# A four-layer graph network on one core: the last chunk's dense products in two column halves, and 0/1 patterns in the last head's first part

## The chip, the core and the metric

The kernel runs on one core of one Trainium2 chip. A core has a matrix engine (TensorE, PE in the profile), a vector engine (VectorE, DVE), an activation engine (ScalarE, ACT), GpSimd (POOL) and SyncE (SP), which here only starts transfers. The metric is the device time of one launch in microseconds. Before the change three runs took 1820.46, 1822.46 and 1822.22 us, median 1822.22.

## The reference, cut to what matters

There are 2708 nodes with 512 features each and a dense 0/1 adjacency matrix. Four layers follow one another, each added to its own input. `lrelu` is a leaky ReLU, `first64` keeps the first 64 neighbors of every row.

```python
def ln_relu(x): return maximum(layernorm(x), 0)

h = ln_relu(x)                                   # layer 0: graph convolution
x = x + relu((adj.T @ h @ W0) * (1/sqrt(degree))[:, None])

h = ln_relu(x)                                   # layer 1: mean of the first 64 neighbors
nb = (first64(adj) @ h) / count
x = x + lrelu(h @ W_line.T + b_line) + lrelu(nb @ W_nb.T + b_nb)

h = ln_relu(x)                                   # layer 2: attention, 8 heads of 64 columns
Wh = h @ W2[head];  f1 = Wh @ a1[head];  f2 = Wh @ a2[head]
e = where(adj > 0, lrelu(f1[:, None] + f2[None, :], 0.2), -9e15)
x = x + concat_over_heads(elu(softmax(e) @ Wh))

h = ln_relu(x)                                   # layer 3: mean of all neighbors
agg = (adj @ h) / degree
x = x + relu(concat(h @ W_self + b_self, agg @ W_nb + b_nb) @ W_comb + b_comb)
```

## The kernel before, in words

**Tiling.** The nodes are cut into 22 chunks of R = 126 rows. The last chunk has 62 rows only; its tiles are loaded twice, into partitions 0 to 61 and again into 64 to 125 (TAIL = 64), so that both copies run through layer norm, transposition and product. The 512 features are four blocks of 128 (NF). The chunks are also taken in groups of 3 or 4 as output columns of the adjacency.

**Layers 0, 1 and 3** have the same two stages. In the dense stage each chunk of the input is loaded, normalized (`norm`, L186), transposed with a ReLU (`relu_T`, L208), and multiplied with the 512x512 weight by `product` (L182): four float32 matmuls, one for each block of features, each 512 columns wide. (Each float32 matmul leaves two records in the trace, so a product is eight.) The product is then cut by `halves` (L258) into a rounded part and the rest[...]. For a full chunk the two parts are two tiles of 126x512; for the last chunk they share one tile, `tail`: the rounded part in rows 0 to 61, the rest in rows 64 to 125, so that one matmul takes both (L366).

The aggregation stage (`aggregate`, L376) multiplies with the adjacency: for each group of output chunks it runs over the 22 input chunks, and the adjacency block for a step (`kt`, made by VectorE in `weight1` L739 and `weight3` L1294) is prepared two steps ahead in three buffers. Layer 0 has one such product (`product0`, L443), layer 1 two (`product1`, L714, with weights `wn` and `wl`), layer 3 two (`nb3`, L1253, and `self3`, L1258; their weights `wfn` and `wfs` are fused from W_nb, W_self and W_comb at the start of the kernel). In layer 1 and 3 the second product does not go into the aggregation: a bias and, in layer 1, a leaky ReLU are applied (`y`), and the rows are stored to DRAM.

**Layer 2.** A dense stage (`product2`, L919) gives Wh, stored to DRAM, and from products with the rows `arow` the two scores f1 and f2. Its first steps run within the aggregation of layer 1. Then ten units of attention follow: head 0 in two parts (1384 and 1324 nodes), heads 1 to 6 whole, head 7 in two parts. Units are numbered from 0, so the first part of the last head is unit 8. Each unit has 22 steps, one for each chunk of neighbors. In a step

- VectorE makes the weights `t` (`make`, L880, one instruction at L886), three steps ahead, in TILES = 4 buffers;
- ScalarE scales the chunk's Wh by exp(f2) (`scale`, L868);
- TensorE multiplies both (`multiply`, L1077): `av`, the weighted sum of Wh, and `sums`, the softmax's denominator. Since an output has only 64 + 1 rows, the nodes are cut into parts that use 32 columns of the array each, four side by side.

The denominator has two forms. In the plain one it is a float32 matmul with exp(f2) itself in one column (`one6`, L876). For 13 of the 22 chunks (BY_SIDE, L795: m mod 5 in 1, 3, 4), where `by_side` (L809) says so, it is a bf16 matmul instead: ScalarE makes a 0/1 pattern `b` of the places where one branch of the leaky ReLU holds (`compare`, L897, a steep sigmoid), and `multiply_sides` (L1092) multiplies it with exact three-part splits of the scores (`parts`). What the other branch adds is counted once for all heads over the same 13 chunks (`mask` L1138, `count_neighbors` L1145, with `parts2`), and the three are put together in layer 3 (`turn3`, L1015). Before the change `by_side` holds for heads 1 to 6.

**Order.** The order is written out by hand and each engine works through its own queue in it. `staged` (L217) interleaves the stages of a dense loop; in the attention, `plan` and `behind` (L1182 to L1222) put other work behind given steps (loading the next head's row, the count, storing results by `evict` L1102, the first chunks of layer 3), and the loop at L1224 emits it all. SyncE starts most loads and stores, ScalarE and GpSimd some. A tile that is allocated in a pool reuses the buffer of an older tile of its tag, and its first write waits until the older one has been read.

The functions of the change:

Of the kernel before, what the change touches and what calls it, by code (L numbers as in the profile page):

```python
# [8 lines left out]
F32 = mybir.dt.float32  # L9
# [11 lines left out]
P = 128  # L21

R = 126
# [21 lines left out]
def fast_layers(  # L45
# [129 lines left out]

    def load_row(pool, src, name, tag=None):

        t = pool.tile([P, D], F32, name=name, tag=tag or name)
        nc.sync.dma_start(t, bass.AP(tensor=src.tensor, offset=src.offset, ap=[[0, P], [1, D]]))
        return t  # L180

    def product(po, lhsT, w, n):  # L182
        for f in range(NF):
            nc.tensor.matmul(po[:n], lhsT[:, f, :n], w[:, f, :], start=(f == 0), stop=(f == NF - 1))  # L184

    def norm(xc, n, scalar=False):  # L186
# [71 lines left out]
    def halves(ring, po, c):  # L258

        if c < NC - 1:  # L260
            t = ring.tile([R, 2, D], F32R, name="halves")
        else:
            t = ring.tile([R, 1, D], F32R, name="tail", bufs=1)
        nc.scalar.copy(t[:, 0, :], po[:R])
        if c < NC - 1:
            nc.vector.tensor_tensor(t[:, 1, :], po[:R], t[:, 0, :].bitcast(F32), ALU.subtract)
        else:
            second = t[TAIL : TAIL + last_rows, 0, :]
            nc.vector.tensor_tensor(
                second, po[TAIL : TAIL + last_rows], second.bitcast(F32), ALU.subtract  # L270
            )
        return t

# [143 lines left out]
    with ExitStack() as ring_ctx:  # L417
# [25 lines left out]
        def product0(c, xc, hT, n):  # L443
            po = ps.tile([P, D], F32, name="h0_ps", tag="ps")
            product(po, hT, w0s, n)
            h0[c] = halves(ring, po, c)
# [267 lines left out]
        def product1(c, xc, hT, size):  # L714
            n = rows(c)
            pn = ps.tile([P, D], F32, name="nb_ps", tag="ps")
            product(pn, hT, wn, size)
            h1[c] = halves(ring, pn, c)
            po = ps.tile([P, D], F32, name="line_ps", tag="ps")
            product(po, hT, wl, size)  # L720
            y = common.tile([P, D], F32, name="y", tag="t", bufs=3)
            nc.vector.tensor_tensor(y[:n], po[:n], bl[:n], ALU.add)
            nc.vector.scalar_tensor_tensor(
                y[:n], y[:n], SLOPE1, y[:n], op0=ALU.mult, op1=ALU.max
            )
            nc.gpsimd.tensor_tensor(xc[:n], xc[:n], y[:n], ALU.add)
            move(nc.scalar, x1[c * R : c * R + n, :], xc[:n])

# [80 lines left out]
    def by_side(u, m):  # L809
        return 0 < units[u][0] < H - 1 and m in BY_SIDE  # L810

# [15 lines left out]
    parts_of = parts[:, : NC * H * 8].rearrange("p (m h k) -> p m h k", h=H, k=8)  # L827
    parts2 = at.tile([R, NC, H, 3], BF16, name="parts2")
    nc.gpsimd.memset(parts2, 0.0)
# [306 lines left out]
    counted, masks = [], {}  # L1136

    def mask(i, j):  # L1138
        m = BY_SIDE[i]
        q = rows(m)  # L1140
        g, k = where[m]
        t = masks[i, j] = common.tile([P, D], F32, name="x", bufs=XBUFS).bitcast(BF16)
        nc.scalar.copy(t[:q, :quarter], vT[g][:q, k, j * quarter : (j + 1) * quarter])

    def count_neighbors(i):  # L1145
        m = BY_SIDE[i]
        q = rows(m)
        if i == 0:
            counted.extend(
                ps.tile([P, 512], F32, name="adj_sums", tag="ps") for _ in pieces(quarter)  # L1150
            )
# [12 lines left out]
        for p, (a, b) in zip(counted, pieces(quarter)):  # L1164
            t = common.tile([P, D], F32, name="out", tag="t", bufs=3)
            for j in range(4):
                own = slice(j * S, j * S + 3 * H)
                nc.scalar.copy(t[own, : b - a], p[own, : b - a])
                nc.sync.dma_start(
                    sumT[7 * H :, j * quarter + a : j * quarter + b], t[own, : b - a]  # L1170
                )
# [72 lines left out]
    with ExitStack() as stack:  # L1244
        ring = stack.enter_context(tc.tile_pool(name="ring3", bufs=NC - 1, reuse_waits="tile"))
        b3 = e3.tile([P, D], F32, name="b3", bufs=1)
        nc.sync.dma_start(
# [5 lines left out]
        def nb3(c):  # L1253
            pn = ps.tile([P, D], F32, name="nb3_ps", tag="ps")
            product(pn, kept3[c][1], wnb, R)
            h3[c] = halves(ring, pn, c)

        def self3(c):  # L1258
            n = rows(c)
            po = ps.tile([P, D], F32, name="self_ps", tag="ps")  # L1260
            product(po, kept3.pop(c)[1], wself, R)
            y = common.tile([P, D], F32, name="y", tag="t", bufs=3)
            ins = nc.vector.tensor_tensor(y[:n], po[:n], b3[:n], ALU.add)
            move(nc.scalar, s3[c * R : c * R + n, :], y[:n])
            return ins.ins
# [713 lines left out]
```

## Time and profile before

The profiled execution took 1820.7 us, of which the span from the first to the last instruction is 1818.8 us. The table splits the span by stages; busy times are sums over the instructions of an engine within that stretch.

| stage | stretch, us | PE busy | DVE busy | ACT busy |
|---|---|---|---|---|
| fused weights, layer 0 | 0 to 376 | 361.3 | 267.4 | 214.9 |
| layer 1 dense | 376 to 541 | 162.2 | 82.4 | 32.1 |
| layer 1 aggregation | 541 to 769 | 225.6 | 144.6 | 6.2 |
| layer 2 dense | 769 to 854 | 84.5 | 67.2 | 51.9 |
| attention, ten units | 854 to 1411 | 551.3 | 538.8 | 388.0 |
| layer 3 dense | 1411 to 1589 | 175.3 | 123.3 | 104.8 |
| layer 3 aggregation | 1589 to 1818 | 221.4 | 84.3 | 0.0 |

How to read it: the difference between a stretch and an engine's busy time is that engine's idle time there. In the attention, TensorE and VectorE are both busy almost throughout; elsewhere VectorE has room. A mean duration of an instruction in the profile is the time from its start to its end, and since matmuls overlap in the array it is longer than the time from one start to the next; the latter is what one more matmul costs. The clock that the chip granted to TensorE, as a mean over the span, was 0.996 of full speed.

### The profile page before, as it was taken

The numbers are of one execution on the slowest core, as the hardware profiler recorded it, in microseconds if no ns is written. First come the engines' busy times: TensorE is split into PE (matmuls) and PEld (weight loads), VectorE is DVE, ScalarE is ACT, GpSimd is POOL, SyncE is SP. The second block draws the span as 40 slices with busy tenths as digits, with TensorE's granted clock in tenths as the row PEclk, the third lists the DMA queues.
The fourth block names the chain that finished last, engine by engine and source line by source line (L and its number), as shares of the span: only waits on it lengthen the run. The fifth ranks groups of instructions, "written<-read, shape, count | busy, mean of one in ns | idle before, by whom it ended". The sixth has DMA issues, their size and how long they took to land.

```text
span 1818.8 us, 30698 instructions
## 1 busy us (share of the span) xinstructions
PE 1781.6 (98%) x11884; PEld 1036.1 (57%) x11884; DVE 1307.9 (72%) x1836; ACT 798.0 (44%) x1542; POOL 245.3 (13%) x241
## 2 busy tenths in 40 slices
PE   9899999999999999999999999999999999999998
PEld 4456777654447887644444344444444454488776
DVE  4942998955546655888999999999998777533334
ACT  2642777722110000156887767767744566400000
POOL 0101333301121111266000000000001222100000
PEclk9999999999999999999999999999999999999999
DMA  7632666635461211343221121122022444313221
GB/s 248 193 114 67 204 208 196 204 76 121 117 149 55 67 54 46 97 147 104 73 61 26 42 62 43 27 61 57 13 65 56 134 131 139 94 38 102 78 69 45
DMA packets 165554, 176.63 MB, mean 97 GB/s; under 512 B 94830, under 2 KB 115792, under 8 KB 164516
## 3 DMA queue, kind: packets, MB, share of 16 engines
q1 hardware_dynamic: 143170, 131.47, 26.2%
q10 hardware_dynamic: 18484, 33.28, 5.4%
q0 software_dynamic: 3744, 9.82, 1.6%
q8 instruction: 96, 1.57, 0.4%
q14 instruction: 60, 0.49, 0.1%
HBM read 111.35 MB, written 55.15 MB: 92 GB/s over the span
## 4 chain that ended last, share of the span: by engine, by line
PE 80%; DVE 9%; issue 4%; DMA 4%; ACT 1%; POOL 1%; SPq 0%; DVEq 0%; ACTq 0%; POOLq 0%
PE acc L368 31%; PE av L1069 19%; PE nb_ps L184 7%; PE sums L1069 6%; PE self_ps L184 4%; PE wh_ps L184 3%; DVE t L886 3%; PE line_ps L184 3%; DVE cum L494 2%; PE h_ps L184 2%; PE hT_ps L212 2%; PE fused_ps L312 2%; DMA x<-x 1%; DMA ai<-in_adj 1%; DVE two L506 1%
## 5 line engine op out<-in xcount | busy, mean ns | idle before, releaser
L886 DVE SCALAR_TENSOR_TENSOR t<-rb,ec,vT 126x2708 f32<-126x2708 f32 (+2 forms) x220 | 532.2, 2472 | 17.6 <-PE sums L1069 9.7
L368 PE MATMUL acc<-halves,kt 126*126 126x512 f32 x1848 | 435.9, 395 | 3.9 <-DVE kt L741 2.3
L1069 PE MATMUL av<-t,whs 126*32 126x451 f32 (+3 forms) x4576 | 436.2, 515 | 0.6 <-DVE ln_mv L191 0.6
L368 PEld LDWEIGHTS acc<-halves,kt 126*126 126x126 f32 x1848 | 342.6, 186 | 93.7 <-DVE kt L741 6.9
L1069 PEld LDWEIGHTS av<-t,whs 126*32 126x32 f32 (+1 forms) x4576 | 158.7, 110 | 207.8 <-issue 188.0
L368 PE MATMUL acc<-halves,ar 126*126 126x512 f32 x924 | 232.7, 405 | 2.1 <-DVE deg L502 1.1
L904 ACT ACTIVATE b<-t,eb 126x2708 bf16<-126x2708 f32 (+1 forms) x78 | 199.1, 2552 | 25.4 <-DVE t L886 25.1
L368 PEld LDWEIGHTS acc<-halves,ar 126*126 126x126 f32 x924 | 169.1, 186 | 52.7 <-issue 7.7
L193 ACT ACTIVATE ln_rs<-ln_mv,eps 126x1 f32<-126x1 f32 x88 | 25.6, 293 | 339.5 <-DVE ln_mv L191 336.5
L741 DVE SCALAR_TENSOR_TENSOR kt<-lastr,index,vT 126x504 fp32r<-126x504 int16 (+3 forms) x154 | 110.6, 729 | 81.0 <-PE acc L368 80.7
L1296 DVE CAST kt<-vT 126x504 fp32r<-126x504 uint8 (+3 forms) x154 | 56.0, 366 | 138.2 <-PE acc L368 138.2
L1069 PE MATMUL sums<-t,whs 126*32 126x338 f32 (+5 forms) x1568 | 139.6, 449 | 2.4 <-ACT out L1110 2.4
L874 ACT ACTIVATE whs<-wh,ef 126x64 f32<-126x64 f32 x220 | 76.8, 349 | 130.6 <-PE sums L1069 66.1
L1036 POOL TENSOR_SCALAR z<-y 126x512 f32<-126x512 f32 x22 | 44.0, 2000 | 662.2 <-DVE y L1029 653.4
L494 DVE TENSOR_TENSOR_SCAN cum<-ai,deg 126x504 int16<-126x504 int32 (+2 forms) x110 | 128.6, 1182 | 0.5 <-DMA ai<-in_adj 0.5
L522 ACT ACTIVATE cum<-cum,limit 126x504 int16<-126x504 int16 (+3 forms) x132 | 88.2, 668 | 58.4 <-DVE deg L502 57.3
L1069 PEld LDWEIGHTS sums<-t,whs 126*32 126x32 f32 (+1 forms) x1568 | 54.9, 109 | 70.0 <-issue 43.7
L189 DVE BATCH_NORM_STATS2 ln_st<-x 126x6 f32<-126x512 f32 x88 | 60.4, 686 | 43.1 <-DMA x<-x 29.1
L184 PE MATMUL h_ps<-w0s,hT 128*126 128x512 f32 x176 | 79.7, 596 | 6.0 <-ACT hT L214 4.7
L184 PE MATMUL nb_ps<-wfn,hT 128*126 128x512 f32 x176 | 81.7, 608 | 2.0 <-ACT hT L214 2.0
L184 PE MATMUL wh_ps<-w2s,hT 128*126 128x512 f32 (+1 forms) x176 | 79.4, 593 | 0.0
L184 PE MATMUL nb_ps<-wn,hT 128*126 128x512 f32 x176 | 79.2, 592 | 0.0
(182 smaller groups left out, 1869.8 us busy)
## 6 DMA issues: line engine op xcount, KB each, us to landing
x<-x SPq DMA_DIRECT2D x105, 252.0 KB
x<-x ACTq DMA_DIRECT2D x84, 252.0 KB
ai<-in_adj SPq DMA_DIRECT2D x84, 249.0 KB
x<-in_x SPq DMA_DIRECT2D x42, 252.0 KB
rb<-rT SPq DMA_DIRECT2D x7, 1332.8 KB
wh<-whd SPq DMA_DIRECT2D x70, 94.5 KB
packed<-two POOLq DMA_DIRECT2D x44, 124.5 KB, 4.3
whd<-wh SPq DMA_DIRECT2D x21, 252.0 KB
```

What stands on the lines that cost most here:

```text
L184: nc.tensor.matmul(po[:n], lhsT[:, f, :n], w[:, f, :], start=(f == 0), stop=(f == NF - 1))
L189: nc.vector.bn_stats(st[:n], xc[:n])
L368: nc.tensor.matmul(acc[:R], weight[:, k * R : (k + 1) * R], parts[:, i, :], start=(m == 0 and i == 0), stop=(m == NC - 1),)
L494: nc.vector.tensor_tensor_scan(cum[:n, :gw], ai[:n, :gw], ai[:n, :gw], 0.0 if g == 0 else deg[:n, m : m + 1], op0=ALU.add, op1=ALU.max,)
L522: nc.scalar.activation(cum[:n, :gw], cum[:n, :gw], AF.Sign, bias=limit[:n], scale=-1.0, accum_out=signs[:n, m, g : g + 1],)
L741: nc.vector.scalar_tensor_tensor(by_chunk(kt, cs), lastr[:, cs[0] * R : (cs[-1] + 1) * R].rearrange("p (c r) -> p c r", r=R), index[:R, m ...
L874: ins = nc.scalar.activation(t[:q, :O], wh.pop((u, m))[:q], AF.Copy, scale=by)
L886: ins = nc.vector.scalar_tensor_tensor(t[:q, : hi - lo], row[h][:q, lo:hi], ec[:q, m, h : h + 1], vT[g][:q, k, lo:hi], op0=ALU.max, op1=AL ...
L904: nc.scalar.activation(b[:q, : hi - lo], weight[s][:q, : hi - lo], AF.Sigmoid, bias=eb[:q, m, h : h + 1], scale=STEEP,)
L1036: nc.gpsimd.tensor_scalar(z, y, 0.0, None, op0=ALU.min)
L1069: nc.tensor.matmul(p[j * S : (j + 1) * S, : b - a], lhsT, rhs[:, part * size + a : part * size + b], start=(s % NC == 0), stop=(s % NC == ...
L1296: nc.vector.tensor_copy(by_chunk(kt, cs), pattern(m, cs))
```

## The change

It has three parts. Everything else is as before.

**Products of the last chunk.** Where a dense product is for the last chunk, `product_of_last` takes only the 62 rows once and cuts the 512 output columns into two halves. The first half is written to rows 0 to 61 of the result, the second to rows 64 to 125, by two matmuls of 256 columns that use different columns of the array. `any_product` chooses; it is used by all six products. What follows is adapted: `halves` for the last chunk clears the `tail` tile and fills it by three copies and two subtractions, `product1` and `self3` do their bias, leaky ReLU and stores in two corners, and `product2` copies two corners.

**Patterns in one more unit.** `by_side` holds for unit 8 as well, for the same 13 chunks. `parts2` now exists in two forms, for the first half of the nodes (heads 1 to 7) and for the second (heads 1 to 6), filled by six copies; the count is cut at the same node as head 7's parts (`fourths`).

**Tiles moved.** The rows `arow` are loaded into a tile of the `weights` pool with tag `w` instead of their own; `rest` uses a tile with tag `t`; `b3` is allocated in the ring of layer 3. By these pools some loads and a few VectorE instructions come at another place in their queues: the `arow` loads go earlier, `wfs` later (behind the last product of layer 2, as `wfn`), `b3` behind the last stores of the attention; one `kt` cast of layer 1 stands ahead of the reductions of `w2s` (L772), and the first three casts of layer 3 ahead of the last `hn` (L203).

```diff
-    def load_row(pool, src, name, tag=None):
-
-        t = pool.tile([P, D], F32, name=name, tag=tag or name)
+    def load_row(pool, src, name, into=None):
+
+        t = into
+        if t is None:
+            t = pool.tile([P, D], F32, name=name)
...
+    HALF = D // 2
+
+    corners = [
+        (slice(0, last_rows), slice(0, HALF)),
+        (slice(TAIL, TAIL + last_rows), slice(HALF, D)),
+    ]
+
+    def product_of_last(po, lhsT, w):
+
+        for f in range(NF):
+            for at_rows, at_cols in corners:
+                nc.tensor.matmul(
+                    po[at_rows, at_cols],
+                    lhsT[:, f, :last_rows],
+                    w[:, f, at_cols],
+                    start=(f == 0),
+                    stop=(f == NF - 1),
+                )
+
+    def any_product(c, po, lhsT, w, n):
+        if c == NC - 1:
+            product_of_last(po, lhsT, w)
+        else:
+            product(po, lhsT, w, n)
...
-        nc.scalar.copy(t[:, 0, :], po[:R])
         if c < NC - 1:
+            nc.scalar.copy(t[:, 0, :], po[:R])
             nc.vector.tensor_tensor(t[:, 1, :], po[:R], t[:, 0, :].bitcast(F32), ALU.subtract)
-        else:
-            second = t[TAIL : TAIL + last_rows, 0, :]
-            nc.vector.tensor_tensor(
-                second, po[TAIL : TAIL + last_rows], second.bitcast(F32), ALU.subtract
-            )
-        return t
+            return t
+        nc.gpsimd.memset(t.bitcast(F32), 0.0)
+        (low, first), (high, other) = corners
+        t = t[:, 0]
+        nc.scalar.copy(t[low, first], po[low, first])
+        nc.scalar.copy(t[low, other], po[high, other])
+        nc.scalar.copy(t[high, other], po[high, other])
+        nc.vector.tensor_tensor(
+            t[high, first], po[low, first], t[low, first].bitcast(F32), ALU.subtract
+        )
+        nc.vector.tensor_tensor(
+            t[high, other], po[high, other], t[high, other].bitcast(F32), ALU.subtract
+        )
+        return t.rearrange("p (i d) -> p i d", i=1)
...
-            product(po, hT, w0s, n)
+            any_product(c, po, hT, w0s, n)
...
-            product(pn, hT, wn, size)
+            any_product(c, pn, hT, wn, size)
...
-            product(po, hT, wl, size)
+            any_product(c, po, hT, wl, size)
...
-            nc.vector.tensor_tensor(y[:n], po[:n], bl[:n], ALU.add)
-            nc.vector.scalar_tensor_tensor(
-                y[:n], y[:n], SLOPE1, y[:n], op0=ALU.mult, op1=ALU.max
-            )
-            nc.gpsimd.tensor_tensor(xc[:n], xc[:n], y[:n], ALU.add)
-            move(nc.scalar, x1[c * R : c * R + n, :], xc[:n])
+            for own in corners if c == NC - 1 else [(slice(0, n), slice(0, D))]:
+                nc.vector.tensor_tensor(y[own], po[own], bl[own], ALU.add)
+                nc.vector.scalar_tensor_tensor(
+                    y[own], y[own], SLOPE1, y[own], op0=ALU.mult, op1=ALU.max
+                )
+                nc.gpsimd.tensor_tensor(xc[own], xc[own], y[own], ALU.add)
+                move(nc.scalar, x1[c * R : c * R + n, own[1]], xc[own])
...
-        return 0 < units[u][0] < H - 1 and m in BY_SIDE
+        return 1 < u < len(units) - 1 and m in BY_SIDE
...
-    parts2 = at.tile([R, NC, H, 3], BF16, name="parts2")
+    parts2 = at.tile([R, len(BY_SIDE), 2, H, 3], BF16, name="parts2")
...
-    ar = [load_row(pp, a, f"arow{i}") for i, a in enumerate((a1, a2))]
+    arows = weights.tile([P, NF, D], F32, name="arows", tag="w")
+    ar = [load_row(None, a, None, into=arows[:, i]) for i, a in enumerate((a1, a2))]
...
-        product(po, hT, w2s.rearrange("p f h o -> p f (h o)"), n)
+        any_product(c, po, hT, w2s.rearrange("p f h o -> p f (h o)"), n)
         wh = pp.tile([R, D], F32, name="wh", bufs=3)
-        nc.scalar.copy(wh[:n], po[:n])
+        if c == NC - 1:
+            for own in corners:
+                nc.scalar.copy(wh[:n, own[1]], po[own])
+        else:
+            nc.scalar.copy(wh[:n], po[:n])
...
-    rest = e3.tile([R, NC, H], F32, name="rest", bufs=1)
...
+        rest = common.tile([P, D], F32, name="rest", tag="t", bufs=3)
+        rest = rest[:R, : NC * H].rearrange("p (m h) -> p m h", h=H)
...
-        heads = slice(1, H - 1)
-        nc.scalar.copy(parts2[:, :, heads], parts_of[:, :, heads, 3:6])
...
-    quarter = N // 4
+        for i, heads in enumerate((slice(1, H), slice(1, H - 1))):
+            for r in sorted({m % 5 for m in BY_SIDE}):
+                ms = [m for m in BY_SIDE if m % 5 == r]
+                src = parts_of[:, r :: 5, heads, 3:6]
+                at_i = [BY_SIDE.index(m) for m in ms]
+                nc.scalar.copy(parts2[:, at_i[0] : at_i[-1] + 1 : 3, i, heads], src)
+
+
+    fourths = [0, cut // 2, cut, (cut + N) // 2, N]
...
-        w = parts2[:q, m].rearrange("p h k -> p (h k)")
-        for p, (a, b) in zip(counted, pieces(quarter)):
+        for n, p in enumerate(counted):
             for j in range(4):
+                a, b = pieces_of(j)[n]
                 nc.tensor.matmul(
                     p[j * S : j * S + 3 * H, : b - a],
-                    w,
+                    parts2[:q, i, j // 2].rearrange("p h k -> p (h k)"),
                     masks[i, j][:q, a:b],
...
-        b3 = e3.tile([P, D], F32, name="b3", bufs=1)
+        b3 = ring.tile([P, D], F32, name="b3", bufs=1)
...
-            product(pn, kept3[c][1], wnb, R)
+            any_product(c, pn, kept3[c][1], wnb, R)
...
-            product(po, kept3.pop(c)[1], wself, R)
+            any_product(c, po, kept3.pop(c)[1], wself, R)
...
-            ins = nc.vector.tensor_tensor(y[:n], po[:n], b3[:n], ALU.add)
-            move(nc.scalar, s3[c * R : c * R + n, :], y[:n])
+            for own in corners if c == NC - 1 else [(slice(0, n), slice(0, D))]:
+                ins = nc.vector.tensor_tensor(y[own], po[own], b3[own], ALU.add)
+                move(nc.scalar, s3[c * R : c * R + n, own[1]], y[own])
```

More of the change, by code (lines that the diff above doesn't have):

```diff
@@ L1130, in split, with pieces_of @@
                     e = rest
-        heads = slice(1, H - 1)
-        nc.scalar.copy(parts2[:, :, heads], parts_of[:, :, heads, 3:6])
-    quarter = N // 4
+        for i, heads in enumerate((slice(1, H), slice(1, H - 1))):
[5 more added lines that the diff above has]
+    fourths = [0, cut // 2, cut, (cut + N) // 2, N]
     counted, masks = [], {}
+    def pieces_of(j):
+        return pieces(fourths[j + 1] - fourths[j])
     def mask(i, j):
@@ L1141, in mask @@
         g, k = where[m]
+        own = slice(fourths[j], fourths[j + 1])
         t = masks[i, j] = common.tile([P, D], F32, name="x", bufs=XBUFS).bitcast(BF16)
-        nc.scalar.copy(t[:q, :quarter], vT[g][:q, k, j * quarter : (j + 1) * quarter])
+        nc.scalar.copy(t[:q, : own.stop - own.start], vT[g][:q, k, own])
     def count_neighbors(i):
@@ L1149, in count_neighbors @@
             counted.extend(
-                ps.tile([P, 512], F32, name="adj_sums", tag="ps") for _ in pieces(quarter)
+                ps.tile([P, 512], F32, name="adj_sums", tag="ps") for _ in pieces_of(0)
             )
-        w = parts2[:q, m].rearrange("p h k -> p (h k)")
-        for p, (a, b) in zip(counted, pieces(quarter)):
+        for n, p in enumerate(counted):
             for j in range(4):
+                a, b = pieces_of(j)[n]
                 nc.tensor.matmul(
                     p[j * S : j * S + 3 * H, : b - a],
-                    w,
+                    parts2[:q, i, j // 2].rearrange("p h k -> p (h k)"),
                     masks[i, j][:q, a:b],
@@ L1163, in count_neighbors @@
             return
-        for p, (a, b) in zip(counted, pieces(quarter)):
+        for n, p in enumerate(counted):
             t = common.tile([P, D], F32, name="out", tag="t", bufs=3)
             for j in range(4):
+                a, b = pieces_of(j)[n]
                 own = slice(j * S, j * S + 3 * H)
@@ L1169, in count_neighbors @@
                 nc.sync.dma_start(
-                    sumT[7 * H :, j * quarter + a : j * quarter + b], t[own, : b - a]
+                    sumT[7 * H :, fourths[j] + a : fourths[j] + b], t[own, : b - a]
                 )
```

## The prediction

> **What bounds the kernel now.** I read the page first: busy shares, slices, the chain that ended last.
>
> ```profile
> span 1818.8 us, 30698 instructions
> ...
> PE 1781.6 (98%) x11884; PEld 1036.1 (57%) x11884; DVE 1307.9 (72%) x1836; ACT 798.0 (44%) x1542; POOL 245.3 (13%) x241
> ...
> PE   9899999999999999999999999999999999999998
> DVE  4942998955546655888999999999998777533334
> ACT  2642777722110000156887767767744566400000
> ...
> PE 80%; DVE 9%; issue 4%; DMA 4%; ACT 1%; POOL 1%; SPq 0%; DVEq 0%; ACTq 0%; POOLq 0%
> ```
>
> TensorE is busy in every slice, and the chain is TensorE for 80%: a TensorE microsecond removed is a microsecond of span, unless another engine stands close behind at that place. VectorE (DVE) does in slices 19 to 31, the attention. So next I took the groups with shapes kept apart (mean ns is latency of one; busy time over count is its share of throughput):
>
> ```profile
> L184 PE MATMUL nb_ps<-wn,hT 128*126 128x512 f32 x176 | 79.2, 592 | 0.0
> L1069 PE MATMUL av<-t,whs 126*32 126x346 f32 x672 | 56.9, 455 | 0.0
> L1069 PE MATMUL sums<-t,whs 126*32 126x346 f32 x336 | 32.1, 453 | 0.0
> L1069 PE MATMUL sums<-b,parts 126*32 126x338 bf16 x288 | 25.0, 306 | 0.0
> L184 PE MATMUL wh_ps<-w2s,hT 128*62 128x512 f32 x8 | 3.6, 598 | 0.0
> ```
>
> A dense product is eight records; in the timeline they start 0.429 us apart, so it costs 3.43 us, for the last chunk too (the last row: 62 columns of weights, same price). Then the timeline of TensorE in the last head's first part (unit 8 of the attention) and, for the price of 0/1 patterns, in an earlier head:
>
> ```profile
> 1341.36 1.35 PE L1069 MATMUL av<-t,whs 126*32 126x346 f32 x16
> 1342.53 0.77 PE L1069 MATMUL sums<-t,whs 126*32 126x346 f32 x8
> 1343.11 0.48 PE L1069 MATMUL av<-t,whs 126*32 126x346 f32 x4
> ...
> 1302.61 0.50 PE L1069 MATMUL sums<-b,parts 126*32 126x338 bf16 x8
> 1302.90 0.59 PE L1069 MATMUL av<-t,whs 126*32 126x451 f32 x4
> ```
>
> A step costs 1.745 us: av 1.165 (sixteen records, to the next start), sums 0.58. The pattern sums of 677 columns cost 0.29, so 346 columns cost 0.146. Last, the two seams of layer 3, its start and its aggregation's start:
>
> ```profile
> 1404.00 1.32 PE L1069 MATMUL av<-t,whs 126*32 126x331 f32 x16 [0.60 <-DVE ln_mv L191]
> 1407.71 0.62 PE L212 MATMUL hT_ps<-ident,hn 126*128 126x126 f32 x4 [1.83 <-DVE hn L203]
> 1411.63 6.09 PE L184 MATMUL nb_ps<-wfn,hT 128*126 128x512 f32 x8
> 1417.56 0.29 PE L1018 MATMUL sums_ps<-mix,sT 80*126 80x16 f32 x2
> ...
> 1588.37 0.68 DVE L1263 TENSOR_TENSOR y<-self_ps,b 62x512 f32<-62x512 f32 x1 [2.12 <-PE self_ps L184]
> 1589.17 1.07 DVE L1296 CAST kt<-vT 126x504 fp32r<-126x504 uint8 x3
> 1589.73 0.47 PE L368 MATMUL acc<-halves,kt 126*126 126x512 f32 x1 [1.39 <-DVE kt L1296]
> ```
>
> At the first TensorE waits for VectorE, and the next product takes 5.93 us instead of 3.43: the clock recorded as granted is half from 1409.65 to 1416.48. At the second TensorE stands 1.39 us because the casts (L1296) come behind the last `y`.
>
> **Part 1: six products in halves (L0 one, L1 two, L2 one, L3 two).** Each becomes sixteen records of 256 columns, two side by side. If they overlap, that is 8 slots of 0.214, 1.72 us: 1.71 saved each, 10.3 in all. No 64-column pair is in this trace; the nearest row is the av row, four 32-column matmuls at once: in the trace's records the four of a slot start within 0.03 us and the next four 0.29 later, where 346/512 of 0.429 is 0.290 for a lone matmul. Four cost what one costs. [...] I take the row. The bounds are 0 (no overlap) and 10.3.
>
> [...] around the 32-column count at 169.5 us the starts are 0.33 and 0.16 apart where 0.23 and 0.055 are usual, and the next matmul again 0.10 late: 0.1 to 0.2 each way. L0, L1 and L3 leave and return once (0.25 each), L2 goes on to 32-column work anyway (0.1): -0.85.
>
> What surrounds them. L0: TensorE has work without a gap from 103 to 311 us, and VectorE's counting is held behind each group's end, so it starts earlier with TensorE: kept in full. L1: behind the products VectorE makes `kt` and reduces `w2s` (2.29 us twice, the first waiting for the weights' load until 547.18). That load starts when `wn` is free, 1.7 us earlier, while TensorE comes 3.2 earlier; the changed order puts one more `kt` ahead of the reduction. Counting the pieces through, TensorE loses 0.3 more; if the load gains nothing, 1.9. Take 0.3. L2: the first attention weights after the product (L886 from 857.44) depend on VectorE work that itself waits for the last product, so it moves along; two copies for one cost 0.2.
>
> Evictions: one ScalarE copy becomes three of 62x256 and one subtraction two, six VectorE ops for three behind `line_ps`, four stores for two on ScalarE's queue (0.31 and 0.36 us to issue each), a 126x512 memset on GpSimd. Each matrix's `tail` is used 21 steps later, over 35 us (in L0 8 us): nothing.
>
> **Part 2: patterns in unit 8.** Thirteen of 22 steps fall from 1.745 to 1.165+0.146 = 1.31: 5.65 saved. The last chunk's pattern sums have 126 rows before and after and 62 within: about 0.12 twice, as at 1330.45 (0.41 to the next start instead of 0.29). Net 5.4.
>
> Who could stop it: VectorE, one 1.66 us `t` per step. Back to back, two starts lie 1.57 apart (1321.78, 1323.35); 22 need 35.0 at 1.59. TensorE will need 13x1.31+9x1.745 = 32.7. VectorE is now paced by TensorE at 1.745, each `t` begun three steps ahead, ready 2.5 us before use. It loses 2.3, so at the end of the unit some 0.5 to 0.9 us of lead is left: just covered. Unit 9 (1.675 a step, `t` 1.51) refills it by step 12, before turn3 begins at step 13, so the VectorE-bound seam above moves as a block. If `t` takes 1.66 start to start, 36.5, the lead is short by 1.3 us. ScalarE gains thirteen sigmoids of 126x1384, each about 1.32 (the 126x1324 exponential of L849 takes 1.26), and drops thirteen 0.31 copies: 1.3 us a step against 1.49, no other work there. The table loads for it exist in earlier heads as in unit 8 (exp before, tanh behind, as now).
>
> The count of neighbors keeps 104 matmuls; 346 columns for 338 cost 26x3 ns = 0.1. `parts2` takes six small copies instead of one (0.535): about 0.3 each, 1.2 more on ScalarE at 877, which idles 0.34+1.19 us until 880. That cover gone, 1.2 would land in the mask stage, where ScalarE is full. I take 0.
>
> **Part 3: moved tiles and loads.** The two `arow` loads go from 762.96 into the L1 aggregation: TensorE does not wait for them now, 0. `wfs` leaves that stage and follows the last product, with `wfn` behind the last GpSimd use of `arows`: five more issues on SyncE's queue of about 0.4 us near 855, ahead of a `wh` load and the 1324-wide `rb`; both have several us: 0, bound 1. `rest` borrows a `t` buffer, back long before the eviction at 899: 0. `b3` now loads behind unit 9's stores, 0.4 us of queue, used 8 us later. With `b3` and `rest` out of that pool, the first casts of layer 3 stand ahead of the last `hn` in VectorE's order: the 1.39 stall goes. They delay `hn` by 1.2, and its transpose has 3.4 to spare.
>
> **Sum.** 10.3 - 0.85 - 0.3 - 0.2 + 5.4 - 0.1 + 1.4 = 15.6. The profiled execution took 1820.7 (span 1818.8 and 1.9 around it), so 1805.1; the median of the runs is 1.5 above it: **1806.6**.
>
> **Rivals.**
> Cover too thin (0.20): VectorE does bind in unit 8 or at the seam, or the half-clock windows fall worse there: 2 to 4 us of the 5.4 go, or one window of 3.41 us costs 1.7 more: about 1810. For it: slices at 9 and the 0.60 and 1.83 waits. Against: the lead counted above.
> [...]
> Halves do not run side by side, so the change doesn't do what it says there (0.06): 10.3 lost, 1817. Against it stands the av row.
> Slower (0.03): in unit 8 `t` waits for its buffer until the sigmoid has read it, so that 1.66 + 1.32 + waits, 3.1 us, becomes the pattern step: 13x1.8 = 23 lost, 1830. It decides beyond 2.5 us a step. Against it: four `t` buffers, and earlier heads keep both engines going the same way.
>
> **How the numbers follow.** All as summed: 0.63, with a range of its own of 1803 to 1809. The range to 1813 takes in the thin cover[...] (0.91 together); its low end, 1802, is the lead-in of layer 3 without its half clock (about 3 us). Faster by over 0.2% (3.6 us, about what this kernel's runs tell from no change) is every case but the last: 0.94 after leaving 0.03 for mishaps that cancel the gain; same 0.03; slower 0.03.
>
> **What would show it.** In after: 62x256 records in pairs, a product under 1.9 us; unit 8's pattern steps at 1.31 and unit 9 starting some 5.5 us earlier relative to unit 8's start; no wait of TensorE on L886's line in unit 8; the first `acc` of layer 3 right behind `self_ps`. Wrong: pairs one after the other, TensorE waiting for `t` in unit 8, longer waits at layer 3's start.

## The result, and the profile after

The changed kernel takes 1804.96 us (median of 4 runs, 1803.19 to 1805.92) against 1821.93 us (4 runs, 1820.46 to 1822.46) of the kernel before: ratio 0.9904, 95% interval 0.9892 to 0.9916. That is 17.0 us less; the forecast was 15.6 less, 1806.6. The profiled executions stand at 1820.7 and 1805.92 us, 14.8 apart, and their spans at 1818.8 and 1804.1.

The page of the changed kernel: span, busy times, and shares of the chain that ended last.

```profile
span 1804.1 us, 30724 instructions
...
PE 1767.0 (98%) x11880; PEld 1039.3 (58%) x11880; DVE 1308.8 (73%) x1842; ACT 815.3 (45%) x1554; POOL 247.3 (14%) x245
...
PE 80%; DVE 10%; issue 4%; DMA 4%; ACT 1%; POOL 0%; SPq 0%; DVEq 0%; ACTq 0%; POOLq 0%
```

TensorE's busy time fell by 14.6 us (1781.6 to 1767.0), as much as the span (14.7). VectorE did the same work as before, ScalarE 17.3 us more (thirteen sigmoids), and neither became the bound over the whole. Next, the groups of TensorE with shapes kept apart:

```profile
L199 PE MATMUL wh_ps<-w2s,hT 128*62 128x256 f32 x16 | 1.9, 385 | 0.0
L199 PE MATMUL nb_ps<-wfn,hT 128*62 128x256 f32 x16 | 1.9, 385 | 0.0
L199 PE MATMUL self_ps<-wfs,hT 128*62 128x256 f32 x16 | 1.9, 379 | 0.0
L1110 PE MATMUL sums<-t,whs 126*32 126x346 f32 x240 | 22.9, 453 | 0.0
L1110 PE MATMUL sums<-b,parts 126*32 126x346 bf16 x48 | 3.9, 309 | 0.0
```

A product of the last chunk is sixteen records in 1.9 us where eight took 3.6. In unit 8, 96 float32 records of the sums (12 steps of 126 rows) gave way to 48 of bf16; the thirteenth step is the last chunk with 62 rows. The timelines of the changed kernel, first unit 8 on TensorE and VectorE, then the start of layer 3, then the start of its aggregation:

```profile
1331.37 2.51 PE L1110 MATMUL av<-t,whs 126*32 126x346 f32 x32
1333.70 0.33 PE L1110 MATMUL sums<-b,parts 126*32 126x346 bf16 x4
1333.85 1.35 PE L1110 MATMUL av<-t,whs 126*32 126x346 f32 x16
...
1328.02 34.70 DVE L923 SCALAR_TENSOR_TENSOR t<-rb,ec,vT 126x1384 f32<-126x1384 f32 x22 [0.15 <-PE sums L1110]
```

```profile
1396.00 1.32 PE L1110 MATMUL av<-t,whs 126*32 126x331 f32 x16 [0.59 <-DVE ln_mv L218]
...
1399.71 0.62 PE L239 MATMUL hT_ps<-ident,hn 126*128 126x126 f32 x4 [1.83 <-DVE hn L230]
...
1402.68 3.70 PE L186 MATMUL nb_ps<-wfn,hT 128*126 128x512 f32 x8
...
1571.25 1.95 PE L199 MATMUL nb_ps<-wfn,hT 128*62 128x256 f32 x16
1573.03 1.90 PE L199 MATMUL self_ps<-wfs,hT 128*62 128x256 f32 x16
1574.85 1.44 PE L403 MATMUL acc<-halves,kt 126*126 126x512 f32 x5
```

In unit 8 the pattern sums take 0.15 us (1333.70 to 1333.85) and TensorE never waits. The row of VectorE holds the fifth to the last `t` of unit 8 and the first four of unit 9; from 1333.05 us on, two starts within unit 8 lie 1.571 us apart without a gap. At the start of layer 3 the two waits (0.59 and 1.83) are where they were, and the product behind them is back at full clock. At the aggregation's start the wait for `kt` is gone.

Lining up the matmuls of both traces gives the time at each landmark:

| from, to | before, us | after, us | gain |
|---|---|---|---|
| start to the last chunk's product in layer 0 | 162.30 | 164.61 | -2.3 |
| that product, to the second matmul behind it | 3.66 | 2.21 | 1.45 |
| from there to the last chunk in layer 1's dense stage | 368.43 | 370.95 | -2.5 |
| two products of layer 1 and what lies behind, to the first `acc` | 7.01 | 3.78 | 3.2 |
| layer 1's aggregation and layer 2's dense stage | 305.08 | 304.76 | 0.3 |
| the product of layer 2 | 7.21 | 5.51 | 1.7 |
| units 0 to 7 | 474.88 | 474.18 | 0.7 |
| unit 8 | 39.25 | 33.44 | 5.8 |
| unit 9 and layer 3's start, to its second neighbor product | 56.40 | 54.63 | 1.8 |
| layer 3's dense stage to the last chunk | 157.08 | 157.18 | -0.1 |
| two products of layer 3 and the stall behind them, to the last `acc` | 229.54 | 224.71 | 4.8 |

(The row of layer 2 includes one full product of 3.6 ahead of the last. 0.39 us of unit 8's gain belong to its last pattern sums, which now lie behind unit 9's first step: 5.4 net.) The losses of 2.3 and 2.5 lie where nothing was changed. A half-clock window lies in each: the record of the granted clock shows half of full speed at 77.9 to 84.7 and at 395.3 to 398.7 us in the profile after, and at 1006.9 to 1010.3 and 1409.7 to 1416.5 us in the profile before, 10.2 us in both. They explain most of the two losses: in the traces without a window there, the first stretch takes 162.3 to 163.7 us and the second 367.7 to 369.6. The windows of before cost less: 0.7 in units 0 to 7 and 2.2 at the start of layer 3 (474.88 and 56.40 us, as against 474.18 and 54.18 in traces without them). With these four amounts left out (-2.3, -2.5, 0.7 and 2.2), the table gives 16.8 us instead of 14.9; the medians of the runs give 17.0.

### The profile page after: what moved, and what is told of

Same layout as the page of the kernel before. It is cut to its first block, busy times and chain, and to the rows that moved or that the text cites. A ratio compares the mean times of both kernels' runs of the same rounds, so it can differ in the third digit from the quotient of the medians.

```text
span 1804.1 us, 30724 instructions
## 1 busy us (share of the span) xinstructions
PE 1767.0 (98%) x11880; PEld 1039.3 (58%) x11880; DVE 1308.8 (73%) x1842; ACT 815.3 (45%) x1554; POOL 247.3 (14%) x245
## 4 chain that ended last, share of the span: by engine, by line
PE 80%; DVE 10%; issue 4%; DMA 4%; ACT 1%; POOL 0%; SPq 0%; DVEq 0%; ACTq 0%; POOLq 0%
PE acc L403 32%; PE av L1110 16%; PE nb_ps L186 7%; PE sums L1110 5%; DVE t L923 5%; PE self_ps L186 4%; PE line_ps L186 4%; PE wh_ps L186 3%; PE h_ps L186 3%; DVE cum L529 2%; PE hT_ps L239 2%; PE fused_ps L347 2%; DMA x<-x 1%; DMA ai<-in_adj 1%; DMA x<-in_x 1%
## 5 line engine op out<-in xcount | busy, mean ns | idle before, releaser
L1110 PEld LDWEIGHTS av<-t,whs 126*32 126x32 f32 (+1 forms) x4576 | 162.4, 110 | 200.7 <-issue 175.2
L941 ACT ACTIVATE b<-t,eb 126x2708 bf16<-126x2708 f32 (+3 forms) x91 | 217.8, 2393 | 34.6 <-DVE t L923 32.9
L1110 PE MATMUL sums<-t,whs 126*32 126x338 f32 (+4 forms) x1464 | 129.6, 447 | 2.7 <-ACT out L1151 2.7
L186 PE MATMUL nb_ps<-wfn,hT 128*126 128x512 f32 x168 | 75.7, 593 | 3.2 <-ACT hT L241 3.2
L523 ACT ACTIVATE ar<-ai 126x504 fp32r<-126x504 int32 (+2 forms) x132 | 74.9, 567 | 3.0 <-DMA ai<-in_adj 3.0
```

What stands on the lines that cost most here:

```text
L523: nc.scalar.activation(ar[:, :gw], ai[:, :gw], AF.Square, accum_out=squares[:R, m, g : g + 1])
L941: nc.scalar.activation(b[:q, : hi - lo], weight[s][:q, : hi - lo], AF.Sigmoid, bias=eb[:q, m, h : h + 1], scale=STEEP,)
L1110: nc.tensor.matmul(p[j * S : (j + 1) * S, : b - a], lhsT, rhs[:, part * size + a : part * size + b], start=(s % NC == 0), stop=(s % NC == ...
```

## Experiments

Every time of the kernel before in this part is from the same chip and the same minutes as the run that it stands beside. The changed kernel's 1804.96 us are from the runs of the result, so differences to it are rougher: the median of the kernel before lay between 1821.71 and 1822.24 us in all these rounds.

**1. Plain products again, the rest kept.**

```diff
     def any_product(c, po, lhsT, w, n):
-        if c == NC - 1:
-            product_of_last(po, lhsT, w)
-        else:
-            product(po, lhsT, w, n)
+        product(po, lhsT, w, n)
```

(`halves`, `product1`, `product2` and `self3` as before the change.)

> The changed kernel with all six products of the last chunk plain again (patterns in unit 8 and moved tiles kept). Theory, by the trace of the changed kernel: the halves are worth 1.45 + 3.2 + 1.7 + 1.65 + 1.75 = 9.8 us, so about 1814.7 us, which is 7.2 under the kernel before. Rival: part of what the trace shows at these places came from the moved tiles, and the halves are worth less[...].

Measured: 1812.63 us (6 runs, 1810.18 to 1817.48), ratio to before 0.9951 (0.9937 to 0.9965), 7.7 above the changed kernel. The trace gives more: between the same landmarks the products cost 1.45 + 3.2 + 1.7 + 1.65 + 1.5 = 9.5 more than in the changed kernel. Times of single runs differ by several microseconds here, so the 7.7 neither contradicts the 9.5 nor decides against the rival. The trace speaks against it: the moved tiles are in this kernel, and yet the products of layer 0, 1 and 2 with what lies behind them take 3.67, 7.00 and 3.58 us, as they did before the change. The next two experiments show what the gain rests on.

**2. The same half-width matmuls, one half after the other.**

```diff
-        for f in range(NF):
-            for at_rows, at_cols in corners:
+        for at_rows, at_cols in corners:
+            for f in range(NF):
                 nc.tensor.matmul(
```

> The changed kernel with the same 96 half-width matmuls in another order: for each product first all four of the first half, then all four of the second. Theory: what is saved is that two neighbors in the queue use different columns of the array at once. In this order only the pair in the middle is different, so a product takes 16 slots of 0.214, 3.43 us or one slot less, and the time goes back by 9.5 to 10.3 us to about 1815 us. Rival: the saving is the 62 columns of weights instead of 126, or TensorE looks further ahead than one instruction: 1805 us, as the changed kernel.

Measured: 1807.23 us (5 runs, 1806.33 to 1809.28), ratio 0.9921 (0.9909 to 0.9934). The theory that only neighbors in the queue run at once falls: 2.3 us were lost, not 10. The rival's 1805 does not come either. Its group of layer 0's product, and the timeline around it:

```profile
L199 PE MATMUL h_ps<-w0s,hT 128*62 128x256 f32 x16 | 2.9, 385 | 0.0
```

```profile
163.22 2.86 PE L199 MATMUL h_ps<-w0s,hT 128*62 128x256 f32 x16
166.01 3.98 PE L403 MATMUL acc<-halves,ar 126*126 126x512 f32 x16
```

The product takes 2.79 us to the next start, where the changed kernel takes 1.88 and experiment 3 takes 3.60. The single records show why: the eight of the first half start at 163.22, 163.48, 163.70, 163.92, 164.13, 164.35, 164.56 and 164.78, and the first of the second half at 164.14, 0.006 behind the fifth. TensorE began the second half while the last three records of the first had not started. (In the program as built the four matmuls of the first half stand ahead of the four of the second, as written.) Where two such products follow one another (layer 1 and 3), the second product's first half begins in the same way beside the first product's second half: in layer 1, records of `line_ps` at 538.28 and 538.50 lie between those of `nb_ps` at 538.22 and 538.44. So only the ends of such a chain are uncovered: two products one after the other take 4.63 us, 3.60 in the changed kernel. In the trace the order costs 2 times 0.91 and 2 times 1.03, 3.9 us, of which the times show 2.3. So the halves run side by side in part only: a lone product gives back about half of what alternating wins.

**3. The same, both halves on the same columns of the array.**

```diff
     corners = [
         (slice(0, last_rows), slice(0, HALF)),
-        (slice(TAIL, TAIL + last_rows), slice(HALF, D)),
+        (slice(0, last_rows), slice(HALF, D)),
     ]
```

(in the order of experiment 2, with `halves` reading rows 0 to 61.)

> As the kernel with the halves one after the other, but both halves are written to rows 0 to 61, so that both use the same columns of the array; 62 columns of weights and 256 columns of data in each matmul as before. Theory: only different columns of the array let two matmuls run at once; now 16 slots of 0.216 us, 3.45 a product, as a plain product: about 10 us more than the changed kernel, 1814 to 1815 us. Rival: the narrower weights make a matmul cheaper by themselves: 1805 to 1807 us.

Measured: 1814.47 us (5 runs, 1810.88 to 1816.36), ratio 0.9955 (0.9941 to 0.9969); 10.2 above a kernel measured beside it that differs from the changed one by small hidden instructions only (1804.24, experiment 6), and 7.2 above experiment 2 (about 6.4 by the products in the two traces).

Group and timeline as above:

```profile
L199 PE MATMUL h_ps<-w0s,hT 128*62 128x256 f32 x16 | 3.7, 382 | 0.0
```

```profile
164.95 3.67 PE L199 MATMUL h_ps<-w0s,hT 128*62 128x256 f32 x16
168.55 2.13 PE L404 MATMUL acc<-halves,ar 126*126 126x512 f32 x8
```

Same matmuls, same order, other columns of the array: 3.6 us a product. The narrow weights alone give nothing (a full-width product took 3.43); the whole gain of part 1 is the use of different columns at once.

**4. Patterns for heads 1 to 6 only, the rest kept.**

```diff
-        return 1 < u < len(units) - 1 and m in BY_SIDE
+        return 0 < units[u][0] < H - 1 and m in BY_SIDE
```

(`parts2` then has heads 1 to 6 in both forms.)

> The changed kernel with patterns for heads 1 to 6 only, as before (halves and moved tiles kept). Theory: unit 8 returns from about 33.4 to 39.2 us, 5.8 more: 1810.7 us, about 11.2 under the kernel before. Rival: VectorE's chain into layer 3 sets the end there, so that a slower unit 8 is partly made up at the seam: 1808 to 1809 us.

Measured: 1812.05 us (5 runs, 1808.87 to 1815.01), ratio 0.9946 (0.9932 to 0.9960); 7.1 above the changed kernel, 5.8 in the trace (unit 8: 39.25 us), or 5.4 with the 0.39 of the last pattern sums. What VectorE did at the seam made up for none of it.

**5. The moved tiles alone: the edits of experiments 1 and 4 together.**

> The changed kernel with plain products and patterns for heads 1 to 6 only: of the change the moved tiles, the count cut at another node and the six copies are left. Theory: the stall of 1.39 us at the first aggregation matmul of layer 3 is gone, little else: 1820.2 to 1820.6 us, 1.4 to 1.7 under before. Rival: the later load of the weights of layer 3 or the longer copies cost it again: 1821 to 1823 us.

Measured: 1819.22 us (21 runs, 1816.10 to 1822.86), ratio 0.9982 (0.9976 to 0.9989), which is 3.3 us under before with an interval of 2.0 to 4.4: more than the 1.4 to 1.7 expected. The trace shows the stall gone:

```profile
1584.02 3.60 PE L186 MATMUL self_ps<-wfs,hT 128*126 128x512 f32 x8
1587.05 5.21 PE L392 MATMUL acc<-halves,kt 126*126 126x512 f32 x20
```

From the last `self_ps` to the end of the aggregation it is 1.66 us shorter than before (1.39 of stall and 0.27 in which matmuls start again after it). Between the first `acc` of layer 1 and the first `wh_ps` it is 0.6 shorter; but traces of kernels that do not differ there spread from 223.9 to 225.6 us. So 1.7 is shown. The granted clock of these runs was 0.9962 as a mean, 0.9958 in the runs of before, which is worth about 0.4 by the fit at the end of this text; what the rest of the 3.3 is stays open.

**6. One more small VectorE instruction a step in unit 8.**

```diff
         t = at.tile([R, N], F32, name="t2", bufs=TILES)
+        if u == len(units) - 2:
+            nc.vector.tensor_tensor(spare, spare, spare, ALU.mult)
```

> The changed kernel with one more VectorE instruction of 126x128 elements ahead of each of the 22 weights t of unit 8, about 0.21 us each (512 columns take 0.69, 8 take 0.15), 4.6 us in all. Theory: VectorE has 1.0 to 1.45 us of lead left at the end of unit 8, and about 0.6 of the load falls into its idle time ahead of the third, fourth and fifth t; the rest, 2.5 us or a little more, delays TensorE in unit 8 and is not made up behind it, since the seam of layer 3 waits for VectorE too: 1807.5 us. Rival: TensorE alone sets the end there: 1805 us. Second rival: all 4.6 show, since the seam is VectorE's: 1809.6 us.

> The same load with patterns for heads 1 to 6 only, to be read against the same kernel without the load (1812.05 us). Theory: TensorE needs 1.745 us a step there, VectorE 1.577 + 0.21 = 1.79, so that 22 steps take 1.0 us from a lead of 3.33: no wait of TensorE in unit 8, and 1812 us as without the load. Rival: the seam is VectorE's alone, so that its work shows wherever it lies: up to 4.6 more, 1816.7 us.

Measured: 1804.24 us (5 runs, 1803.72 to 1808.28) with the patterns and 1812.31 (5 runs, 1811.31 to 1814.29) without. Neither number says anything on the lead: the 22 instructions depend on nothing in unit 8 and had been put at 766 to 790 us, as the rows of their tile show. The first kernel serves as a second measurement of the changed one (1804.24 beside 1804.96).

**7. Wider `t` in unit 8.** Here the load is in the instruction itself, so it cannot move. 200 columns more are computed and not read.

```diff
+        to = hi + 200 if u == len(units) - 2 else hi
...
-            row[h][:q, lo:hi],
+            row[h][:q, lo:to],
```

> The changed kernel in which VectorE makes 1584 columns of t in each step of unit 8 instead of 1384; the 200 more are not read. (In the run with one more small instruction a step those 22 instructions had been put at 766 to 790 us, outside unit 8, so it told nothing of the lead.) By 0.53 us for 512 columns the 200 cost 0.21 a step, 4.6 in 22. Theory: the first three fall into idle time, the lead of 1.0 us takes its part, and TensorE is held up by 3.0 us in unit 8, which is not made up behind it: 1807.9 us. Rival: TensorE alone sets the end, VectorE has more room than the lead shows: 1805 us. Second rival: the seam at layer 3 is VectorE's and all of it shows: 1809.5 us.

> The same wider t in unit 8, with patterns for heads 1 to 6 only, against 1812.05 us without it. Theory: VectorE's step of 1.785 stands against 1.745 of TensorE, 0.9 us in 22 steps out of a lead of 3.33: no wait, 1812 us. Rival: the seam is VectorE's alone: up to 1816.7 us.

Measured: 1808.47 us (5 runs, 1807.60 to 1811.16) with the patterns, 3.5 above the changed kernel; 1812.51 (5 runs, 1809.66 to 1814.99) without them, against 1812.05. VectorE and TensorE with the patterns:

```profile
1323.64 44.48 DVE L924 SCALAR_TENSOR_TENSOR t<-rb,ec,vT 126x1584 f32<-126x1584 f32 x26 [0.90 <-PE av L1111]
...
1345.27 1.37 PE L1111 MATMUL av<-t,whs 126*32 126x346 f32 x16 [0.25 <-ACT whs L911]
1347.05 1.37 PE L1111 MATMUL av<-t,whs 126*32 126x346 f32 x16 [0.26 <-ACT b L942]
1350.61 1.37 PE L1111 MATMUL av<-t,whs 126*32 126x346 f32 x16 [0.29 <-ACT whs L911]
```

TensorE waits about 0.26 us at a step from 1345 us on. (The releaser named is ScalarE's small instruction; it had long been done, and the one that came last is `t`, on which VectorE works without a gap.) Unit 8 takes 35.83 us instead of 33.44: 2.4 of the 4.6 us show and 2.2 were room: the lead, and VectorE's idle time ahead of the first `t`, which fell from 2.3 to 1.4 us. The 2.4 are still there at the last `acc`, beside 3.0 of a half-clock window at 1413 us. Without the patterns unit 8 takes 39.25 as before. So the cover of part 2 was real and about 2 us thick, and VectorE is the next limit in unit 8.

**8. Patterns in unit 9 too, for six chunks.**

```diff
-        return 1 < u < len(units) - 1 and m in BY_SIDE
+        own = BY_SIDE[:6] if u == len(units) - 1 else BY_SIDE
+        return u > 1 and m in own
```

(`parts2` then has head 7 in its second form too, cleared for the other seven chunks.)

> The changed kernel with 0/1 patterns also in unit 9, for the first 6 of the 13 chunks (those below 10). Theory: TensorE saves 6 times 0.555 - 0.14 = 2.5 us. VectorE needs 1.51 a step against 14.3 / 10 = 1.43 of TensorE in these ten steps, takes 0.8 from a lead of 1.4, and has it back by step 13, where layer 3's first work is put in; its idle time in unit 9 (0.165 a step) is what is used up. So the seam comes 1.5 to 2.5 us earlier: 1802.5 to 1803.5 us. Rival: VectorE or the sigmoid's place in ScalarE's queue binds, and nothing is won or it turns slower: 1805 to 1808 us.

Measured: 1804.87 us (4 runs, 1803.39 to 1806.52), ratio 0.9906 (0.9890 to 0.9921): as the changed kernel. TensorE did gain 2.49 us up to the first `sums_ps`, and then stood at the seam:

```profile
1392.96 1.32 PE L1111 MATMUL av<-t,whs 126*32 126x331 f32 x16 [1.72 <-DVE ln_mv L218]
1396.67 0.62 PE L239 MATMUL hT_ps<-ident,hn 126*128 126x126 f32 x4 [1.83 <-DVE hn L230]
```

The first wait grew from 0.59 to 1.72, which takes 1.1 of the 2.5. A half-clock window of 6.8 us lay behind the second at 1397 us in this trace and took more than the rest: from the start of unit 9 to the second neighbor product it is 55.5 us, 54.6 in the changed kernel.

**9. Patterns in unit 9, and layer 3's first work two steps earlier.**

```diff
-        behind(len(steps) - at_step, fn, c)
+        behind(len(steps) - at_step - 2, fn, c)
```

> The changed kernel with patterns in unit 9 for the six chunks below 10, and the first work of layer 3 (loads, the turns of chunks 0 to 2, the ELU and norm of chunk 0) put two steps earlier into unit 9. Theory: patterns in unit 9 alone won 2.5 us up to step 13 and gave it back at the seam, where TensorE waits for VectorE's norm and ScalarE's transposed copy (0.6, 1.83 and 3.2 us in the changed kernel); with the chain two steps earlier, one to three of these microseconds go: 1801.5 to 1803.5 us. Rival: VectorE is full in those steps, the chain only pushes the last t back, and TensorE waits for them instead: 1805 us or more.

Measured: 1805.16 us (4 runs, 1804.84 to 1806.99), ratio 0.9908 (0.9893 to 0.9922): no better. The rival's number was right, and in part its reason. TensorE's waits, and two rows of VectorE ahead of the first of them:

```profile
1389.29 1.32 PE L1111 MATMUL av<-t,whs 126*32 126x331 f32 x16 [1.72 <-DVE ln_mv L218]
1393.85 0.62 PE L239 MATMUL hT_ps<-ident,hn 126*128 126x126 f32 x4 [2.12 <-DVE hn L230]
1411.58 4.26 PE L186 MATMUL nb_ps<-wfn,hT 128*126 128x512 f32 x6 [3.66 <-ACT hT L241]
```

```profile
1385.43 0.69 DVE L1083 SCALAR_TENSOR_TENSOR z<-z,th 126x512 f32<-126x512 f32 x1 [1.47 <-ACT z L1082]
1387.56 1.59 DVE L924 SCALAR_TENSOR_TENSOR t<-rb,ec,vT 126x1324 f32<-126x1324 f32 x1
```

The three waits are 7.5 us together, 5.6 in the changed kernel (0.59, 1.83 and 3.22), and from the start of unit 9 to the second neighbor product it is 54.5 us as against 54.6. So at least 1.9 of the 2.5 us taken from TensorE in unit 9 come back as waits, and moving the block as a whole does not shorten it. But VectorE is not full there, as the rival had it: the first matmul of the three waits for the `t` that ends at 1389.15, and this `t` stands behind `z` in VectorE's queue, ahead of which VectorE idles 1.47 us until ScalarE has done its part. In the changed kernel the same 1.47 us stand at 1390.67. The order within the block thus holds the `t` back; a `t` put ahead of `z` was not tried.

**10. `b3` back in its old pool.**

```diff
-        b3 = ring.tile([P, D], F32, name="b3", bufs=1)
+        b3 = e3.tile([P, D], F32, name="b3", bufs=1)
```

> The changed kernel with b3 alone back in its old pool. Its last reader is the last y of layer 3, and the first casts of the aggregation then stand behind that y in VectorE's order, as before the change. Theory: that order is the whole of the stall of 1.39 us at the first aggregation matmul, which comes back: 1806.3 us, and nothing else moves. Rival: the load of b3, which is then issued earlier, or rest matters: 1805 us.

Measured: 1811.29 us (6 runs, 1802.38 to 1815.79), a spread too wide to tell 1.4 us. The trace tells it:

```profile
1579.31 1.90 PE L199 MATMUL self_ps<-wfs,hT 128*62 128x256 f32 x16
1583.26 9.02 PE L403 MATMUL acc<-halves,kt 126*126 126x512 f32 x31 [2.05 <-DVE kt L1349]
...
1582.70 1.07 DVE L1349 CAST kt<-vT 126x504 fp32r<-126x504 uint8 x3
```

The casts stand behind the last `y` again and TensorE waits 2.05 us for them. So the place of `b3` alone makes this stall. It costs more than itself here: from the last neighbor product to the last `acc` it is 228.36 us, 224.71 in the changed kernel, since a half-clock window begins right behind the stall. Five more such windows stand in the 1814.0 us of this trace.

None of these versions beats the changed kernel by more than the runs spread.

## Why the prediction held, step by step

**Products in halves** (forecast 10.3 - 0.85 = 9.45): 9.5 by the trace. Pairs start 0.006 us apart and the next pair 0.216 later, where a lone half-width record takes the same 0.216 (experiment 3); two at once cost what one costs, as the row of four 32-column matmuls had said. The switch to these matmuls and back cost 0.09 ahead of the product, 0.10 behind it and 0.10 once more in layer 0, 0.29 where 0.25 was assumed. That the halves should stand next to each other in the queue was not in the sum; apart, they keep about half of the gain (experiment 2).

**Layer 1's `kt` and reduction** (0.3 lost): 0.26 gained in the trace of the changed kernel; where equal kernels differ by up to 1.7 it can't be told. **Layer 2's copies** (0.2): nothing; the gain there is 1.7.

**Unit 8** (5.4): 5.8, or 5.4 with the sums that slipped behind unit 9's start. The step in the working that was off is the lead: `t` was said to be ready 2.5 us before its use; its end lies 3.33 us before in the trace of before, and 1.0 to 1.45 in the last three steps after, where 0.5 to 0.9 had been forecast. That forecast did not follow from its own terms (2.5 less the 2.3 that VectorE loses leaves 0.2); with 3.33 the sum leaves the 1.0 that was measured, so the right number was luck in part. At 1.571 us from start to start, twenty-two `t` need 34.6 us (35.0 forecast), and a sigmoid took 1.44 us (1.32 forecast), still under the mean step of 1.49. The rival of the thin cover was 2.2 us of VectorE's work away (experiment 7). The rival that ends slower, a `t` held by its sigmoid, did not come: a step with a pattern costs 1.31 us, not 3.1.

**Count, copies, moves of loads** (0.1 and 0): nothing to be seen in units 0 to 7, whose 0.7 us are those of a half-clock window; the six copies took 1.09 us on ScalarE while TensorE went on.

**Layer 3's stall** (1.4): 1.39 and 0.27 behind it. The cause given, the pool of `b3` and `rest`, narrows to `b3`.

**What was not priced.** The half-clock windows in the profile of before were taken as part of the kernel, and the median was put 1.5 above the profiled execution, as it had been before. The profile after has windows elsewhere, and its execution, 1805.92 us, was the slowest of four (1805.1 had been forecast for it). Two things can have put the median 1.6 us below 1806.6, and the runs do not tell them apart. The moved tiles measured 3.3 where 1.1 (1.4 less 0.3) stood in the sum, with a cause known for 1.7. And the granted clock of the four runs was 0.997 as a mean, as against 0.9958 in the 27 runs of before of experiments 1, 2, 4 and 5, which is worth about 1.3 us by the fit below.

## What to carry to other kernels

For a product of few rows, try cutting its output columns in two and putting the halves on different columns of the array: here one of 62 rows took about half the time (1.88 us instead of 3.43) with the halves in alternation; one after the other (2.79 us) they still kept about half of the gain. Before an engine's work is cut, read the lead of the engine that feeds it, from the end of one instruction to the start of its user: it says how much of the gain is covered (here 3.3 us of lead covered the 2.3 that were lost, with 1.0 left). What is taken just ahead of a seam that waits for another engine can come back as waiting there (1.9 of 2.5 us in experiment 9), although what was taken a unit earlier did not (experiment 4). A tile's pool decides when the first instructions of the next stage may be placed: one bias row in the wrong pool held three casts and cost 1.7 us.

## What the runs showed of the hardware that was not expected

In experiment 2 TensorE began a matmul on other columns of the array while earlier ones in its queue had not started: the second half's first record started 0.006 us behind the fifth of eight of the first half, with three of that half's eight, 0.64 us of starts, still to come.

The profiles before and after have four stretches of half clock up to the last `acc`: 3.41 us from 1006.88 and 6.83 us from 1409.65 in the one, 6.83 us from 77.88 and 3.41 us from 395.31 in the other. In the 3.41 us ahead of them TensorE idled 2.26, 1.47, 2.51 and 2.28 us. Experiment 10 has the same at its stall (busy times of PE, PEld, DVE, ACT and POOL, then the granted clock):

```profile
1580.44:1583.86 3.42, 1.37 (x11) 0.77 (x8) 3.06 (x11) 0.22 (x1) 0.00 (x0) 1.00 0.16 33
1583.86:1587.27 3.41, 3.41 (x10) 2.65 (x9) 1.89 (x11) 0.00 (x0) 0.00 (x0) 0.50 0.76 231
```

TensorE idled 2.05 us in the first stretch and had half the clock in the second. A long wait was not always followed by one: in the profile after TensorE waits 3.22 us ahead of 1414.07 us, in the profile before 2.60 us ahead of 76.60 us, and the granted clock is 1.00 from 1396 to 1420 us in the one and from 70 to 90 us in the other. What decides between the two is not shown, nor whether fewer such windows are a part of what the change won.

A fit over all runs, with a level of its own for each kernel, gives 1.1 us for each 0.001 of mean clock; the clock accounts for about four tenths of the variance among runs of one kernel.
